# A later place for the last quarter's residual and result units of one column phase in a two-layer directional-scan kernel

## The chip, the cores and the metric

The kernel runs on one core of one Trainium2 chip. The metric is the device time of one launch in microseconds. The profile is of one execution on the chip, and all times within it are counted from the start of its span.

## What is computed

The input x has 32 images, 48 channels, 64 rows and 128 columns in float32. Two layers follow one another. Each is `x = x + conv(gn(x))`, where `gn` normalises each image over 16 groups of channels, and `conv` is four scans one behind the other. A scan goes over the rows downward, then upward, and then over the columns to the right and to the left. Each of its steps adds to the next row (or column) a 5-tap convolution of the one before it:

```python
def _conv1d(x, w, b):                      # over one row or column: 48 channels in, 48 out, 5 taps
    y = jax.lax.conv_general_dilated(x, w, window_strides=(1,), padding=[(2, 2)], ...)
    return y + b[None, :, None]
def step(w, b):
    def f(carry, inp):
        nxt = inp + _conv1d(carry, w, b)
        return (nxt, nxt)
    return f
_, d_rest = jax.lax.scan(step(down_w, down_b), d0, xs[1:])        # down the rows
_, u_rest = jax.lax.scan(step(down_w, down_b), u0, seq)           # and up
_, r_rest = jax.lax.scan(step(right_w, right_b), r0, ws[1:])      # along the columns
_, l_rest = jax.lax.scan(step(left_w, left_b), l0, R[Ww - 2::-1]) # and back
...
x = x + _L0_conv_ref(_gn(x), ...)
x = x + _L1_conv_ref(_gn(x), ...)
```

## The kernel before

**Groups and phases.** The 32 images are four groups of eight. A phase is one pair of scans: "rows" (down and up, 126 steps) for one group, or "cols" (right and left, 254 steps) for a pair of groups at a time. Twelve phases follow one another, numbered from 0:

```python
PHASES = (
    ("rows", 0, 0), ("rows", 0, 1), ("cols", 0, 0), ("rows", 0, 2),
    ("rows", 1, 0), ("rows", 0, 3), ("cols", 0, 1), ("rows", 1, 1),
    ("rows", 1, 2), ("rows", 1, 3), ("cols", 1, 0), ("cols", 1, 1),
)
```

The triple is kind, layer, and group or pair. Phase 6 is the column phase of layer 0 for the second pair (groups 2 and 3). Phase 7 is the row phase of layer 1 for group 1, and phase 8 that of layer 1 for group 2.

**A step.** `step` (L889, L898) issues nine matmuls on TensorE into three PSUM tiles, and three instructions on VectorE that add bias and input. The three tiles are the three thirds `o` of the 384 values (48 channels of eight neighbouring lines) in which a row or column is laid over the 128 partitions. A step needs the one before it. The names of the PSUM tiles tell the phase: `step_01l` is phase 6's scan to the left, `step_11d` phase 7's scan downward, `step_11u` its scan upward, `step_12d` phase 8's scan downward.

**Memory.** The tile `arena` has three slots and four staging tiles of 128 x 2048 (1 MB each). A row phase uses two slots of 32 rows. A column phase needs four quarters of 32 columns, `quarter(k, j)`, in three slots: j = 3 and j = 0 share a slot, and j = 0 goes to device memory for a while (`spill_unit`). A quarter consists of six units of 1 MB, `UNITS[i] = (o, half)`; the half is the group of the pair.

**What goes beside a column phase's end.** After the scan to the left has passed a quarter, each unit of layer 0 goes through: `load_residual` (DMAs on SP's queue, `arena<-xin`, three or four for 1 MB), `add_residual` (L824, GpSimd), `keep_result` (SP's queue, `mid<-arena`), and the statistics for the next layer's normalisation. These are `bn_stats` on VectorE (L573, eight to a unit) for half 0, and sums on ScalarE (L597, L600, L603) for half 1. The four staging tiles take the residuals in turn, so the load of unit u uses the tile of unit u - 4. When the last unit is through, `scaling` turns the statistics into scale and offset: a chain of small instructions spread over steps, with a square root on ScalarE (L469) and a reciprocal on VectorE (L479) ten steps behind it. It runs once for group 2 and, 20 steps later, once for group 3.

**What goes beside a row phase.** Rows come in four blocks of 16. `take_rows` reads them from `mid` (SP's queue, `arena<-mid`; 12, 16 and 12 DMAs for the thirds o = 0, 1, 2 of a block, 1 MB each), and `scale_rows` (L722) applies scale and offset on ScalarE, 24 activations to a block. In phase 7 block reads are due 30, 14 steps before and 2, 18 steps after its start (thirds three steps apart), and the scaling 13 steps before and 3, 19, 35 after. Rows go back to memory as `upb<-arena`. Phase 7 also loads the weights of layer 1's column scans (`more_weights`: memsets on GpSimd L323, then DMAs `taps`, `early`, `wleft`) from its 50th step on.

**Order.** All of this is put on an agenda by `at(t, fn, ...)`, where t counts steps of the whole program. Between the steps the agenda is emptied up to the current step, and `in_order` chains each instruction to the one before it on the same engine. So the agenda fixes the order on every engine and every queue; it does not fix the time, since an engine or queue goes on as soon as what it waits for is there. In `plan_cols`, `left` is the step at which the scan to the left begins and `end = left + 127` the phase's end, which is the next phase's start. The agenda of the units is made in the loop over `direct`, from the list `units` of (step, quarter, unit).

Of the kernel before, what the change touches and what calls it, by code (L numbers as in the profile page):

```python
# [119 lines left out]
def kernel(  # L120
# [631 lines left out]
    def quarter(k, j):  # L752
        return slot[slots(k)[j % 3]].rearrange("p (o s n) -> p s o n", s=2, o=NG)
# [214 lines left out]
    def at(t, fn, *args):  # L968
        agenda.append((t, len(agenda), fn, args))

    def spread(t, gen, every):


        def go(t):
            if next(gen, "end") != "end":
                at(t + every, go, t + every)
                agenda.sort(key=lambda a: a[:2])

        at(t, go, t)
# [64 lines left out]
    def follows(k):  # L1044

        _, layer, pair = PHASES[k]
        return PHASES[k - 1] == ("rows", layer, 2 * pair + 1)

    def plan_cols(k, t0, prev):
        _, layer, pair = PHASES[k]  # L1050
        n = 2 * NG
        after = prev == "cols"
        if follows(k):
            at(t0 + 1.2, hold_queue, k)
        for i in range(n):
            if follows(k) and UNITS[i][1] == 1:
                other = nc.gpsimd
                at(t0 - 31 + i, load_unit, k, 0, i, 4, NH, 0, E8, other)
                at(t0 - 13 + i, load_unit, k, 0, i, 2, 4, 0, E8, other)
                at(t0 - 6 + i / n, load_unit, k, 0, i, 1, 2, 0, E8, other)  # L1060
            else:
                early = 30 if after else 46 if k == 2 else 70
                at(t0 - early + 2 * i, load_unit, k, 0, i)
            if follows(k):
                queue = nc.sync if UNITS[i][1] else nc.scalar
                at(t0 + 1.5, load_unit, k, 1, i, 0, NH, 0, E8, queue)
            else:
                at(t0 + (3 if after else -24 + 2 * i), load_unit, k, 1, i)
            at(t0 + (38 if after else 8) + 2 * i, load_unit, k, 2, i)
            at(t0 + 33 + 2 * i, spill_unit, k, i, False)  # L1070
            at(t0 + 50 + 2 * i, load_unit, k, 3, i)
        final = k == len(PHASES) - 1
        left = t0 + W - 1
        end = left + W - 1
        for i in range(n):

            t = left + 64 + 2 * i if layer == 0 else left + 39.5 + 4.5 * i
            at(t, spill_unit, k, i, True)
        units = []
        for n_done, j in enumerate((3, 2, 1, 0)):  # L1080
            every = 4.5
            if j == 0 and PHASES[k + 1 if not final else k][0] == "rows":
                every = 7
            units += [(left + 34 + 32 * n_done + every * i, j, i) for i in range(n)]
        stats = None
        if layer == 0:
            stats = ResultStatsV(f"r{2 * pair}"), ResultStatsA(f"r{2 * pair + 1}")
        tiles = [stage[:, i] for i in range(4)]
        if layer:
            tiles += spare_tiles[0 : 2 if final else 1]  # L1090
        n = len(tiles)
        direct = [u for u in units if not (final and u[1] == 0)]

        for u, (t, j, i) in enumerate(direct):
            nat = tiles[u % n]
            o, half = UNITS[i]
            if u < n:
                at(left + 16, load_residual, k, j, i, nat)
            if layer == 0:
                if u >= n:  # L1100
                    at(direct[u - n][0] + 3, load_residual, k, j, i, nat)
                at(t, add_residual, k, j, i, nat)
                at(t + 4, keep_result, k, j, i)
                unit = quarter(k, j)[:, half, o]
                if half == 0:
                    for b in range(GB):
                        at(t + 5 + b, stats[0].take, j, o, unit, b)
                else:
                    at(t + 1, stats[1].take, j, o, unit)
            else:  # L1110

                at(t, add_residual, k, j, i, nat)
                at(t + 2.5, permute_unit, k, j, i, nat, (nc.gpsimd, nc.scalar, nc.scalar))
                if final or j not in HELD:
                    at(t + 4.5, store_result, k, j, i, nat)
                else:
                    at(t + 4.5, hold_result, j, i, nat)
                if final and j == 1:
                    at(t + 4.7, load_residual, k, 0, i, last_tiles(k)[i])

                if u >= 2 and u - 2 + n < len(direct):
                    at(t + 4.6, load_residual, k, *direct[u - 2 + n][1:], tiles[(u - 2) % n])
        if layer == 0:
            t = units[-1][0] + 14
            g = 2 * pair
            spread(t, scaling(f"r{g}", 1, g, stats[0], r_masks, 8), 1)
            spread(t + 20, scaling(f"r{g + 1}", 1, g + 1, stats[1], r_masks, 8), 1)
        if layer:

            at(left + 10, nc.scalar.copy, junk[:, BN - 1 :], quarter(k, 3)[:, 0, 0, RUN - 1 : RUN])  # L1130
        if layer and not final:
            todo = [(j, half, e) for j in HELD for half in range(2) for e in range(E8)]
            for n, what in enumerate(todo):
                at(end + 63 + 1.9 * n, let_result, *what)
        if final:
            at(end + 4, last_results, k)

    def last_tiles(k):

        s = slot[slots(k)[2]].rearrange("p (i n) -> p i n", i=2 * NG)  # L1140
        return [s[:, i] for i in range(2 * NG)]
# [13 lines left out]
    for k, (kind, layer, _) in enumerate(PHASES):  # L1155
        (plan_rows if kind == "rows" else plan_cols)(k, starts[k], PHASES[k - 1][0])
# [259 lines left out]
```

## Time and profile before

| | |
|---|---|
| runs shown | 4172.45, 4185.11, 4185.0 us; median 4185.0 us |
| profiled execution | 4178.27 us; its span 4176.5 us |
| mean granted TensorE clock | 0.989 |
| phase 6, scan to the left | first matmul 2107.8 us, last 2355.9 us |
| phase 7, scan downward | first matmul 2356.1 us, last 2496.3 us |
| phase 7, scan upward | first matmul 2496.4 us, last 2626.1 us |
| phase 8, scan downward | first matmul 2626.2 us, last 2751.6 us |
| issue to landing (median) | `arena<-xin` of 384 KB, 10.0 us; `arena<-mid` of 96 KB, 3.1 us; `mid<-arena` of 1024 KB, 10.3 us |

A view names an instruction as line, engine, operation and "tile written <- tiles read". PE is TensorE, PEld its weight loads, DVE VectorE, ACT ScalarE, POOL GpSimd, and SPq the queue of DMAs that SyncE issues. A bracket at the end of a timeline's line is the engine's idle time before it and what ended it. The view of waits gives total time, number and longest. A row of the view by stretches has, for each engine, its busy time and number of instructions, then the granted TensorE clock, the busy share of the DMA engines and their GB/s. A line of SPq in the timeline shows when a group of DMAs was issued, not when the data landed.

### The profile page before, as it was taken

Reading aid. Unit: us, or ns where it says so; the run is one execution under the profiler, and the core shown is the slowest. Engines: PE = TensorE matmul, PEld = TensorE weight load, DVE = VectorE, ACT = ScalarE, POOL = GpSimd, SP = SyncE. Lnnn points to the kernel's source line nnn. Section 1 sums busy time; section 2 is a strip of 40 time slices with the busy share of each in tenths; the row PEclk is TensorE's granted clock in tenths of the full one; section 3 lists DMA queues with packets and bytes.
Section 4 is the critical chain, followed back from the end, with each engine's and each line's share of the span. In section 5 each row is a group of like instructions: output and inputs, shape, how many; then the busy total and the mean of one; then the engine's idle time right before and its main releaser. Section 6 shows DMA issues by size and latency. Waiting matters only on the chain. (4 is left out here: it accounts for less than half of the span.)

```text
span 4176.5 us, 90284 instructions
## 1 busy us (share of the span) xinstructions
PE 4076.3 (98%) x36724; PEld 4045.9 (97%) x36724; DVE 2133.2 (51%) x6501; ACT 1287.0 (31%) x2525; POOL 787.2 (19%) x737
## 2 busy tenths in 40 slices
PE   8999999999999999999999989999999999999994
PEld 6999999999999999999999989999999999999994
DVE  5454444456654454444457654444444444444444
ACT  6844000536964543000016853413000002200122
POOL 3520010434321000010023410000000005610353
PEclk9999999999999999999999999999999999999997
DMA  9987669669979989258419968849379019999799
GB/s 294 235 178 119 111 125 213 208 161 254 217 190 163 174 157 157 37 103 201 92 45 267 188 143 139 140 74 148 57 136 212 2 51 239 287 268 155 146 236 195
DMA packets 2206496, 680.57 MB, mean 163 GB/s; under 512 B 2008464, under 2 KB 2157184, under 8 KB 2179968
## 3 DMA queue, kind: packets, MB, share of 16 engines
q1 hardware_dynamic: 2062096, 582.09, 68.0%
q10 hardware_dynamic: 141424, 87.19, 8.8%
q0 software_dynamic: 2560, 5.51, 0.5%
q8 instruction: 289, 4.73, 0.5%
q14 instruction: 127, 1.04, 0.1%
HBM read 397.77 MB, written 295.14 MB: 166 GB/s over the span
## 5 line engine op out<-in xcount | busy, mean ns | idle before, releaser
L722 ACT ACTIVATE arena<-arena,offset,scale 128x256 f32<-128x256 f32 (+2 forms) x840 | 581.3, 790 | 318.8 <-DMA arena<-mid 125.0
L824 POOL TENSOR_TENSOR arena<-arena 128x2048 f32<-128x2048 f32 x80 | 362.9, 4549 | 1447.1 <-PE step_10l L889 462.3
L659 POOL COPY arena<-arena 128x256 f32<-128x256 f32 x332 | 196.8, 659 | 455.6 <-DMA arena<-in_x 287.3
L597 ACT ACTIVATE early<-arena 128x256 f32<-128x256 f32 x192 | 129.7, 675 | 441.6 <-POOL arena L824 435.7
L889 PE MATMUL step_01r<-arena,early 128*128 128x128 f32 x2286 | 251.8, 274 | 6.8 <-DMA arena<-arena 5.5
L889 PEld LDWEIGHTS step_01r<-arena,early 128*128 128x128 f32 x2286 | 250.8, 185 | 7.7 <-issue 5.8
L889 PE MATMUL step_00r<-arena,early 128*128 128x128 f32 x2286 | 251.2, 274 | 6.9 <-DMA arena<-arena 5.4
L889 PEld LDWEIGHTS step_00r<-arena,early 128*128 128x128 f32 x2286 | 250.5, 185 | 7.6 <-issue 5.7
L889 PE MATMUL step_00l<-arena,wleft 128*128 128x128 f32 x2286 | 249.2, 272 | 0.0
L889 PE MATMUL step_11r<-arena,early 128*128 128x128 f32 x2286 | 249.2, 273 | 0.0
L889 PEld LDWEIGHTS step_11r<-arena,early 128*128 128x128 f32 x2286 | 248.7, 184 | 0.4 <-DVE arena L898 0.3
L889 PEld LDWEIGHTS step_00l<-arena,wleft 128*128 128x128 f32 x2286 | 248.7, 184 | 0.0
L889 PE MATMUL step_11l<-arena,wleft 128*128 128x128 f32 x2286 | 248.5, 272 | 0.0
L889 PE MATMUL step_10l<-arena,wleft 128*128 128x128 f32 x2286 | 248.5, 272 | 0.0
L889 PE MATMUL step_01l<-arena,wleft 128*128 128x128 f32 x2286 | 248.4, 272 | 0.0
L889 PE MATMUL step_10r<-arena,early 128*128 128x128 f32 x2286 | 248.4, 272 | 0.0
L889 PEld LDWEIGHTS step_11l<-arena,wleft 128*128 128x128 f32 x2286 | 248.4, 184 | 0.0
L889 PEld LDWEIGHTS step_10l<-arena,wleft 128*128 128x128 f32 x2286 | 248.4, 184 | 0.0
L889 PEld LDWEIGHTS step_10r<-arena,early 128*128 128x128 f32 x2286 | 248.4, 184 | 0.0
L889 PEld LDWEIGHTS step_01l<-arena,wleft 128*128 128x128 f32 x2286 | 248.4, 184 | 0.0
L282 ACT COPY early<-arena 128x1 f32<-128x1 f32 x2 | 0.4, 191 | 704.2 <-DVE arena L898 704.2
L846 ACT COPY arena<-arena 128x256 f32<-128x256 f32 x172 | 99.8, 657 | 365.5 <-POOL arena L824 249.2
(200 smaller groups left out, 7080.5 us busy)
## 6 DMA issues: line engine op xcount, KB each, us to landing
xin<-arena SPq DMA_DIRECT2D x91, 512.0 KB, 4.1
arena<-in_x SPq DMA_DIRECT2D x18, 2048.0 KB, 11.9
arena<-xin SPq DMA_DIRECT2D x96, 384.0 KB, 10.0
arena<-mid SPq DMA_DIRECT2D x384, 96.0 KB, 3.1
upb<-arena SPq DMA_DIRECT2D x192, 192.0 KB, 3.9
arena<-upb SPq DMA_DIRECT2D x96, 384.0 KB, 12.5
arena<-xin SPq DMA_DIRECT2D x180, 192.0 KB, 4.3
mid<-arena SPq DMA_DIRECT2D x32, 1024.0 KB, 10.3
```

Source lines behind the costliest of these rows:

```text
L282: fn(*args)
L597: nc.scalar.activation(junk[:, 0:n], view[:, b], AF.Identity, accum_out=self.sum[:, i, j : j + 1])
L659: copy(dst[:, r, q], src[:, r0 + r, q])
L722: nc.scalar.activation(args[0], args[0], AF.Identity, bias=args[2], scale=args[1])
L824: eng.tensor_tensor(unit, unit, nat, ALU.add)
L846: copy(by_w(perm)[:, a], src[:, a])
L889: nc.tensor.matmul(part(whole(ps[o])[0:m], -s), weights[:, i, at : at + m], part(src(i), s), start=seen[o] == 1, stop=seen[o] == left[o],)
```

## The change

Only the last quarter (j = 0) is concerned, and only where a row phase follows and `pair` is 1: phase 6. Its units' adds had been due 7 steps apart from step `left + 130`, which is 3 steps after the phase's end. Now they are due 6 steps apart from `end + 29`. What hangs on that step moves along: the keeping 4 steps later, the statistics, and the chain that makes scale and offset. A load into a staging tile was due 3 steps after the tile's previous use; now it is due no earlier than 21 steps ahead of its own add.

```diff
         units = []
         for n_done, j in enumerate((3, 2, 1, 0)):
-            every = 4.5
+            first, every = left + 34 + 32 * n_done, 4.5
             if j == 0 and PHASES[k + 1 if not final else k][0] == "rows":
-                every = 7
-            units += [(left + 34 + 32 * n_done + every * i, j, i) for i in range(n)]
+                first, every = (end + 29, 6) if pair else (first, 7)
+            units += [(first + every * i, j, i) for i in range(n)]
...
             if layer == 0:
                 if u >= n:
-                    at(direct[u - n][0] + 3, load_residual, k, j, i, nat)
+                    at(max(direct[u - n][0] + 3, t - 21), load_residual, k, j, i, nat)
                 at(t, add_residual, k, j, i, nat)
                 at(t + 4, keep_result, k, j, i)
...
         if layer == 0:
             t = units[-1][0] + 14
             g = 2 * pair
             spread(t, scaling(f"r{g}", 1, g, stats[0], r_masks, 8), 1)
             spread(t + 20, scaling(f"r{g + 1}", 1, g + 1, stats[1], r_masks, 8), 1)
```

The last piece is unchanged and shown because its step follows from `units`. In steps after phase 7's start, for the six units:

| | before | after |
|---|---|---|
| loads | -17, -12.5, -8, -3.5, +6, +13 | +8, +14, +20, +26, +32, +38 |
| adds | +3, +10, +17, +24, +31, +38 | +29, +35, +41, +47, +53, +59 |
| kept | +7, +14, ... +42 | +33, +39, ... +63 |
| scale and offset of groups 2 and 3 begin | +52, +72 | +73, +93 |

On SP's queue the order of the entries around phase 7's blocks is thereby (b3/1 is the second third of block 3):

```
before: load0 ... b2/0 load1 ... b2/1 load2 b2/2 ... load3 ... b3/0 b3/1 load4 keep0 b3/2 load5 keep1 b4/0 keep2 b4/1 b4/2 keep3 keep4 keep5 weights
after:  b2/0 ... b2/1 b2/2 ... b3/0 b3/1 load0 b3/2 load1 b4/0 load2 b4/1 b4/2 load3 load4 keep0 load5 keep1 keep2 weights keep3 weights keep4 keep5
```

The "..." in the two lines are units of the quarter before, in the same place in both.

On ScalarE the statistics of the three units of half 1 stood after block 2, after block 3 and after block 4 of the scaling, and now all stand after block 4. The square root for group 3 stood ahead of phase 8's first scaling and now stands behind its second block.

## The prediction

> **What bounds the kernel now.** I read the page first, then TensorE's waits, then the chain behind its longest wait: VectorE, ScalarE, the queue of SP.
>
> ```profile
> span 4176.5 us, 90284 instructions
> PE 4076.3 (98%) x36724; PEld 4045.9 (97%) x36724; DVE 2133.2 (51%) x6501; ACT 1287.0 (31%) x2525; POOL 787.2 (19%) x737
> ```
>
> TensorE is busy for 98%, so a gain can only come from the 100 us in which it isn't, and from time at half clock. TensorE's waits say where those are (columns: total, times, longest):
>
> ```profile
> PE step_11d L889 <- DVE arena L898: 10.9, 1, 10.9
> PE step_00d L889 <- DVE arena L898: 8.4, 4, 3.9
> PE step_01r L889 <- DMA arena<-arena: 5.5, 1, 5.5
> ```
>
> The longest single one lies in step_11d: the downward scan of phase 7, which is the phase right behind the column phase that the diff edits. VectorE's timeline there:
>
> ```profile
> 2419.26 0.35 DVE L898 SCALAR_TENSOR_TENSOR arena<-step_11d,bd,arena 128x128 f32<-128x128 f32 x1 [0.79 <-DMA arena<-mid]
> 2430.76 0.61 DVE L898 SCALAR_TENSOR_TENSOR arena<-step_11d,bd,arena 128x128 f32<-128x128 f32 x2 [11.15 <-ACT arena L722]
> ```
>
> This is row 32 (31 steps of 2.0 us after 2356.5), the first row of the third block of 16 rows. VectorE waits for ScalarE's scaling of that block. ScalarE's timeline, three groups of eight, one for each third o of the block:
>
> ```profile
> 2398.73 6.06 ACT L722 ACTIVATE arena<-arena,offset,scale 128x256 f32<-128x256 f32 x8
> 2407.90 6.07 ACT L722 ACTIVATE arena<-arena,offset,scale 128x256 f32<-128x256 f32 x8 [3.11 <-DMA arena<-mid]
> 2424.74 5.98 ACT L722 ACTIVATE arena<-arena,offset,scale 128x256 f32<-128x256 f32 x8 [10.78 <-DMA arena<-mid]
> ```
>
> So ScalarE itself waits for the row reads. SP's queue (start, time over which the group was issued) shows what those stand behind:
>
> ```profile
> 2363.22 1.78 SPq L271 DMA_DIRECT2D arena<-xin  x4
> 2365.11 11.17 SPq L271 DMA_DIRECT2D arena<-mid  x12
> 2376.32 2.03 SPq L271 DMA_DIRECT2D mid<-arena  x2
> 2378.75 4.03 SPq L271 DMA_DIRECT2D arena<-xin  x4
> 2382.82 1.02 SPq L271 DMA_DIRECT2D mid<-arena  x2
> 2383.96 22.36 SPq L271 DMA_DIRECT2D arena<-mid  x28
> 2406.41 1.32 SPq L271 DMA_DIRECT2D arena<-xin  x3
> 2407.83 0.38 SPq L271 DMA_DIRECT2D mid<-arena  x1
> 2408.32 13.39 SPq L271 DMA_DIRECT2D arena<-mid  x12
> ```
>
> The x12 at 2408.32 is the late third (o = 2, 1 MB), landed at 2424.6. One after another, without a pause, stand residual loads (xin, 1 MB a unit), kept results (mid<-arena, 1 MB) and row reads. The queue is the bound of this stage: in these stretches the DMA engines are 95% and 92% busy, and after the stall TensorE's clock has dropped as well:
>
> ```profile
> 2356.00:2418.00 62.00, 61.94 (x561) 61.60 (x561) 39.52 (x111) 50.46 (x92) 22.63 (x5) 1.00 0.95 176
> 2418.00:2436.00 18.00, 7.07 (x44) 6.90 (x43) 2.36 (x7) 11.07 (x22) 6.13 (x4) 0.63 0.92 188
> ```
>
> (PE, PEld, DVE, ACT, POOL, then clock, DMA share, GB/s.)
>
> **What the stall costs.** Step 32 is late by 10.9 us. Steps 33 and 34 then take 3.94 and 2.78 us by VectorE's timeline, not 2.0: 1.9 + 0.8 at half clock. Together 13.6 us. Cross-check: step_11d's last VectorE instruction starts 138.9 us after its first, step_12d's 124.2; of these 14.7 us, 1.3 belong to two steps that carry statistics matmuls, which stay. The Trainium skill (TensorE: Matmul & The Clock Gate, the clock-gate part) has the half-rate state end after about 3.4 us of sustained work; that would cost half of 3.4, 1.7 us, so 12.6 in all. The trace has 2.7 after the stall; I take the trace.
>
> **The change part by part.** It touches only the last quarter (j = 0) of phase 6; pair 0 keeps every 7 steps from the old start, layer 1's column phases do not meet the condition. Nothing is added or removed; six units (6 MB in, 6 MB out) move in every queue. The "+8" below are steps after phase 7's start, 2356.5.
>
> *Loads (20 DMAs on SP).* From -17, -12.5, -8, -3.5, +6, +13 to +8, +14, +20, +26, +32, +38. The max() alters no load of the other quarters: there the tile-free time is at most 20 steps ahead of the use. Ahead of the late third stood five of these loads and the first kept unit; in the new order of SP one load stands there. So 5 MB leave. Price of 1 MB of these kinds in a stretch without row reads:
>
> ```profile
> 2258.30 5.03 SPq L271 DMA_DIRECT2D arena<-xin  x3
> ...
> 2284.57 23.44 SPq L271 DMA_DIRECT2D arena<-mid  x28
> ```
>
> Between these starts three loads and three kept units went out: 26.3 us / 6 = 4.4 us per MB. The six MB of row reads at 2499.83, alone in the queue, took 49.3 us, 8.2 per MB. The Trainium skill (DMA: Bandwidth & Descriptors, Specifications) gives a ceiling of 435 GB/s, an estimated 2.4 us per MB. By the page 5 MB are 12 us: the third lands at 2412.6, is scaled by 2418.7, and is needed at 2419.6, so the stall would only just close, with 1 us to spare. By the row they are 22 us: landed 2402.6, scaled by 2408.7, 11 us to spare. I take the row, because it is this queue with these shapes; the page's figure is the low end. ScalarE is no new bound: block 2 ends at 2381.6 if not held by data (2363.5 + 24 x 0.75), block 3 needs 18 us.
>
> *Fourth block (rows 48 on).* Needed at step 48, now 2356.5 + 47 x 2.0 = 2451, where before it had the stall's 14 us of grace. Its last third landed at 2457.9. Ahead of it now stand three loads instead of six loads and three kept units: 6 MB less, 26 us, so 2432, scaled by 2438: 13 us to spare by the row; 14 us less by the page, 2443.5, scaled by 2449.6, so 1 us. This is next in line after row 32.
>
> *Adds (6 on GpSimd, 4.55 us each).* From +3..+38 to +29..+59. GpSimd has idle time of 7 to 21 us around each now. Queued behind are the two weight memsets (1.06 us each; those weights are first used three phases on) and the copy of row 63 (needed at the end of phase 7). Nothing, as long as the loads come in.
>
> *Statistics.* VectorE takes 24 bn_stats (0.62 us) at +34.., +46.., +58.., in the idle half of a 2.0 us step as before (three 0.35 us instructions there). They wait for adds, and the scan is queued behind them. Third use: step +58 is at 2472; its load now goes out behind block 4 and one more load, about 2432 + 9 + 7 to land = 2448, added by 2457 with one add ahead of it. 15 us to spare; the first two have about 20. ScalarE's three units (13.5 us each) leave the gaps between the blocks' scaling and follow block 4: 2438 + 40 = 2478; their next reader comes at +93, about 2542. Nothing.
>
> *Kept results (8 DMAs on SP).* From +7..+42 to +33..+63. One now stands behind the first set of weight DMAs (25 + 5), two units behind the second, where before all stood ahead of both. Phase 8's first read waits for the last even unit to land: bound 0 (hidden) to about 8 us (their median landing), in a queue that is then 60 us ahead of need (below). Nothing on the path.
>
> *Coefficients of rows 2 and 3.* Both chains start 21 steps later (+73, +93). The first coefficients were ready at 2534.7; minus 13.6 plus 21 steps, 2563. Phase 8's scaling began at 2572.0 before, held by the second square root, so it isn't later. The second square root now stands behind two blocks of phase 8's scaling on ScalarE (48 x 0.743 = 36 us, so until 2599), and VectorE's reciprocal that needs it moves from 2591 to 2591 - 13.6 + 42 = 2619. 20 us to spare.
>
> *Sum.* 10.9 + 2.7 = 13.6 us gained, nothing given back. The profiled execution took 4178.3 us (span 4176.5): 4164.7. The median of the three runs is 4185.0, 6.7 above it, the lowest 4172.5 below it. If the median run has the same stall, 4171.4; if its excess is a longer stall of this same queue, 4164.7. I say 4168.
>
> **The rivals.**
> *The wait moves to row 48, or only shrinks (0.14).* For it: block 4 has no grace any more, and the DMA engines stay saturated. Were the row reads slow for themselves and not by what is queued ahead, block 4 would land at 2457.9 as before, be scaled by 2464 and stop row 48 for 13 us: no change, 4178 to 4185. Half of that gives a gain of 7. Against it: reads alone run at 8.2 us per MB, 13.4 among residuals.
>
> *The square root behind the scaling (0.12), slower.* Place: VectorE's reciprocal for row 3's coefficients at step 3 of phase 8, in front of every scan step. If block 2 of phase 8 is scaled after 2619, each us later is one us of TensorE's time, plus 2.7 for the clock. It decides against the change from 2619 + 11 = 2630 on, that is, if that block lands after about 2624. For it: the kept units now stand right ahead of these reads, and other waits could add to it. Against it: those reads landed by 2550.8. A landing 25 us beyond that point: about 4178 + 25 = 4203.
>
> *No effect in a run (0.05)*, if runs outside the profile don't stall here at all: the lowest run, 4172.5, is 12.5 under the median, nearly the price of this stall. Then 4172 to 4185.
>
> **How the numbers follow.** The stall gone: 0.69, 4158 (lowest run less 13.6 = 4158.9) to 4172. Moved, shrunk or without effect: 0.19, 4172 to 4186. Slower: 0.12, 4190 to 4205. A measurement of this kernel tells about 0.3%, 12.5 us, from no change: faster is under 4172.5. The main case lies there, 0.69; the second within 0.3%, 0.19; slower 0.12. The range, 4156 to 4181, holds the main case and more than half of the second, 0.8 in all, with 2 us below the lowest sum for the spread between runs.
>
> **What would show it.** Right: TensorE's waits hold no step_11d of over 2 us; the clock in 2418 to 2436 stays at 1.00; step_11d spans about 125 us; row reads of phase 7 follow each other in SP's queue with at most one load among the third block; ScalarE scales three blocks without statistics between them. Wrong: a wait of step_11d at about 2451 (row 48), of VectorE on GpSimd's adds at about 2425, 2449 or 2472, or of step_12d within its first steps on ScalarE's square root.

## The result, and the profile after

The changed kernel takes 4165.7 us in the median (4160.2 to 4172.8, 7 runs); the kernel before, timed with it, 4185.0 us (4172.5 to 4192.4, 7 runs). The ratio is 0.9966, with a 95% interval of 0.9952 to 0.998: 14 us less, between 8 and 20. (The two medians lie 19 us apart, near the upper end of that.) Two more measurements of the same file, each beside new runs of the kernel before, gave 0.9970 (0.9959 to 0.9981) both times.

The profiled execution took 4172.8 us, 5.5 less than the profiled one of before, and not 14. The reason has to be sorted out first. TensorE's instructions of phase 7's scan downward (with the shortest, median and longest matmul in ns, and the first and last start in us):

```profile
L889 PE MATMUL step_11d<-arena,early x1134: 266/275/377, 2364.0 to 2489.4; 128*128 128x128 f32 x126, 128*96 128x120 f32 x63
```

The upward scan behind it:

```profile
L889 PE MATMUL step_11u<-arena,early x1134: 266/275/356, 2489.5 to 2620.5; 128*128 128x128 f32 x126, 128*96 128x120 f32 x63
```

The scan downward spans 125.4 us; before it was 140.2 (2356.1 to 2496.3). The upward one spans 131.0, before 129.7, since the 1.3 us of the first statistics matmuls moved into it. From phase 7's first matmul to its last it is 256.5 us against 270.0: **13.5 us gained**.

But phase 7 began 7.9 us later (2364.0, not 2356.1). The change touches nothing ahead of phase 6's last 17 steps, and in the profiles of kernels that are alike up to there this start lies anywhere from 2355.3 to 2364.0. The 7.9 us arise far ahead of the change, in two scans: from its first matmul to the next scan's, phase 2's scan to the right (`step_00r`) takes 257.5 us, before 252.5, and phase 3's scan downward (`step_02d`) 136.0, before 132.8. In the nine profiles in which both are untouched they take anything from 252.5 to 259.5 and from 127.7 to 136.0, whichever kernel it is, and every other scan ahead of phase 7 varies by less than 1 us. From phase 7's end to the end of the span the two profiles agree within 0.1 us. So the two profiled executions' times hide more than half of the gain, and the stretch that the change touches shows it.

No wait of TensorE in step_11d is left. Where its longest waits were, the list now has (total, times, longest; 7.4 us of the second line is a wait of phase 3, which was 4.1 us in the profile before):

```profile
PE step_00d L889 <- DVE arena L898: 9.7, 4, 4.0
PE step_02d L889 <- issue: 8.3, 2, 7.4
PE step_00r L889 <- DMA arena<-arena: 6.0, 3, 4.7
PE step_01r L889 <- DMA arena<-arena: 5.9, 1, 5.9
```

SP's queue in the same stage, over the times at which each group was issued:

```profile
2346.85 18.36 SPq L271 DMA_DIRECT2D arena<-mid  x28
2365.31 5.02 SPq L271 DMA_DIRECT2D mid<-arena  x4
2370.44 19.77 SPq L271 DMA_DIRECT2D arena<-mid  x28
2390.26 1.37 SPq L271 DMA_DIRECT2D arena<-xin  x3
2391.74 11.48 SPq L271 DMA_DIRECT2D arena<-mid  x12
```

The row reads of blocks 2 and 3 (x28 is two thirds, x12 the last) now have only one residual load among them. ScalarE scales block 2 and the first two thirds of block 3 in one go, and then waits for the rest:

```profile
2371.44 29.83 ACT L722 ACTIVATE arena<-arena,offset,scale 128x256 f32<-128x256 f32 x40
2405.12 6.06 ACT L722 ACTIVATE arena<-arena,offset,scale 128x256 f32<-128x256 f32 x8 [3.85 <-DMA arena<-mid]
...
2442.28 6.05 ACT L722 ACTIVATE arena<-arena,offset,scale 128x256 f32<-128x256 f32 x8 [1.75 <-DMA arena<-mid]
```

Block 3's last third is scaled from 41.1 us after phase 7's first matmul (2405.12 - 2364.0); before it was 68.6. (Six further profiles have the same order of entries around phase 7, namely those of the last two sets below; there it is scaled from 44.0 to 46.1 us on. So one profile tells this time to some us only.) Row 32 is due there after about 63.5 us, so this scaling must start by 57.5. The last line is the last third of block 4, done at 2448.3, some 11 us before row 48 needs it; in the six further profiles it is done 6 to 7 us before. The DMA engines are as busy as before, and the clock stays up:

```profile
2364.00:2426.00 62.00, 61.94 (x562) 61.60 (x561) 31.01 (x95) 49.09 (x75) 9.11 (x3) 1.00 0.96 163
2426.00:2444.00 18.00, 17.99 (x165) 17.83 (x164) 11.93 (x33) 7.78 (x11) 4.50 (x1) 1.00 0.96 142
```

These are the two stretches shown for before, moved by phase 7's later start. The second now has 18.0 us of TensorE in 18, not 7.1. The DMA engines move no more GB/s than before (163 and 142, then 176 and 188), so the wait did not go because transfers became faster; they came in another order.

### The profile page after: what moved, and what is told of

Read it like the earlier page. It is cut to its first block, busy times and chain, and to the rows that moved or that the text cites. A ratio compares the mean times of both kernels' runs of the same rounds, so it can differ in the third digit from the quotient of the medians.

```text
span 4171.0 us, 90280 instructions
## 1 busy us (share of the span) xinstructions
PE 4073.2 (98%) x36724; PEld 4042.8 (97%) x36724; DVE 2135.8 (51%) x6501; ACT 1287.2 (31%) x2525; POOL 786.9 (19%) x737
## 5 line engine op out<-in xcount | busy, mean ns | idle before, releaser
L889 PE MATMUL step_00r<-arena,early 128*128 128x128 f32 x2286 | 252.5, 274 | 9.8 <-DMA arena<-arena 6.0
L846 ACT COPY arena<-arena 128x256 f32<-128x256 f32 x172 | 99.6, 657 | 363.0 <-POOL arena L824 272.8
## 6 DMA issues: line engine op xcount, KB each, us to landing
arena<-xin SPq DMA_DIRECT2D x96, 384.0 KB, 10.2
```

The source lines that it names most:

```text
L846: copy(by_w(perm)[:, a], src[:, a])
L889: nc.tensor.matmul(part(whole(ps[o])[0:m], -s), weights[:, i, at : at + m], part(src(i), s), start=seen[o] == 1, stop=seen[o] == left[o],)
```

## The experiments

Each kernel was timed beside the kernel before on the same chip. "After phase 7's first matmul" is counted in each kernel's own profile.

**How much each MB costs, and of which kind: loads back in their old place.** From the changed kernel:

```diff
-                    at(max(direct[u - n][0] + 3, t - 21), load_residual, k, j, i, nat)
+                    at(direct[u - n][0] + 3, load_residual, k, j, i, nat)
```

> The changed kernel, but the loads of the last quarter's residuals go out where they did before (3 steps after their tile's previous use): four of them ahead of blocks 2 and 3 of phase 7's row reads. Adds, kept units and statistics stay late, so load 5 and the first kept unit (2 MB) have left the place ahead of block 3's last third, and four loads (4 MB) are back in it. Theory (each MB ahead of a row read delays it by 4.4 us, whatever it is): that third lands 8.8 us earlier than in the kernel before, the wait of step_11d for row 32 is about 2 us, not 10.9, and not 0; no wait at row 48. Rival (only loads count, or only what is issued after the phase's start counts): wait near 10.9, or none and the third landed as early as in the changed kernel. Time: between the two kernels, 8 to 13 us under the kernel before.

Measured: 4171.9 us, ratio 0.9983 (0.9973 to 0.9993). TensorE's waits in phase 7, and the scaling of block 3's last third:

```profile
PE step_11d L889 <- DMA arena<-mid: 2.2, 1, 2.2
```

```profile
2420.70 6.02 ACT L722 ACTIVATE arena<-arena,offset,scale 128x256 f32<-128x256 f32 x8 [1.47 <-DMA arena<-mid]
```

That is 59.9 us after the first matmul (2360.8), 8.7 earlier than in the kernel before, where 8.8 were expected, and the wait is 2.2 us, where 2 were. (The view of TensorE's waits names a DMA here; VectorE's timeline has 2.46 us of waiting for ScalarE's scaling at this place.) The ratio allows a gain of 3 to 11 us; 8 to 13 were expected.

**Only the kept units late.** From the kernel before:

```diff
-                at(t + 4, keep_result, k, j, i)
+                late = j == 0 and pair
+                at(end + 33 + 6 * i if late else t + 4, keep_result, k, j, i)
```

> The kernel before, in which the last quarter's six kept units of phase 6 alone are written late (33 to 63 steps into phase 7); loads, adds and statistics as before. One MB leaves the place ahead of block 3's last third, three the place ahead of block 4. Theory: the third lands 4.4 us earlier, the wait for row 32 is 6 to 7 us and still costs the clock; 4 to 5 us faster. Rival (the writes are what holds up the row reads): the wait falls to under 2 us, and the whole 13 us are gained.

Measured: 4178.2 us, ratio 0.999 (0.9981 to 1.0). TensorE waits once in phase 7:

```profile
PE step_11d L889 <- DVE arena L898: 4.6, 1, 4.6
```

```profile
2420.47 6.00 ACT L722 ACTIVATE arena<-arena,offset,scale 128x256 f32<-128x256 f32 x8 [5.43 <-DMA arena<-mid]
```

The last third is scaled from 62.3 us after the first matmul (2358.2), 6.3 earlier. So one MB brought more than the 4.4 expected, and the wait is 4.6, not 6 to 7; but the writes alone are not what held the reads up. The scan downward spans 132.9 us, 7.3 less than before; the ratio of the times allows a gain of 0 to 8 us.

**Half the delay.** From the changed kernel:

```diff
-                first, every = (end + 29, 6) if pair else (first, 7)
+                first, every = (end + 15, 6) if pair else (first, 7)
```

> The changed kernel with half the delay: adds from 15 steps into phase 7, not 29; loads then at -6, 0, +6, +12, +18, +24 steps, kept units from +19, statistics of half 1 on ScalarE at +22 and +34, ahead of block 4's scaling. Theory: three MB less ahead of block 3's last third, no wait for row 32; but only two MB less ahead of block 4, and two units of statistics (27 us of ScalarE) between block 3's and block 4's scaling: block 4 is scaled at about 2463 us (counted as in the profile before), needed at 2451: the wait moves to row 48, about 10 us plus the clock's 2.7, and 0 to 3 us are gained. Rival (any delay past the phase's start is enough): no wait, as fast as the changed kernel, 13 us under the kernel before.

Measured: 4181.5 us, ratio 0.9998 (0.9989 to 1.0008): the whole gain is gone. TensorE's waits in phase 7, and VectorE's timeline where it stands:

```profile
PE step_11d L889 <- DVE arena L898: 10.1, 1, 10.1
```

```profile
2466.90 0.61 DVE L898 SCALAR_TENSOR_TENSOR arena<-step_11d,bd,arena 128x128 f32<-128x128 f32 x2 [10.28 <-ACT arena L722]
```

This is not row 32, which no longer waits (its last third is scaled from 54.4 us on, first line below), but row 48: 105.6 us after the first matmul at 2361.3. The wait moved to the next block, at its expected size. ScalarE scaled block 4 there without a break behind two units of statistics:

```profile
2415.67 6.05 ACT L722 ACTIVATE arena<-arena,offset,scale 128x256 f32<-128x256 f32 x8 [8.86 <-DMA arena<-mid]
...
2449.02 17.85 ACT L722 ACTIVATE arena<-arena,offset,scale 128x256 f32<-128x256 f32 x24
```

So two possible causes stood in the same place, and one more kernel takes one of them away.

**Half the delay, but ScalarE's statistics behind block 4.** From the kernel just shown:

```diff
-                    at(t + 1, stats[1].take, j, o, unit)
+                    late = j == 0 and pair
+                    at(max(t + 1, end + 36) if late else t + 1, stats[1].take, j, o, unit)
```

> The kernel with half the delay (adds from 15 steps into phase 7), in which only ScalarE's statistics of the last quarter's units go behind block 4's scaling. There the wait had moved to row 48 (10.1 us), with both ScalarE's statistics and the row reads ahead of it. Theory (the queue alone decides): block 4's last third lands as late as before (about 96 us after phase 7's first step), its scaling ends 6 us later, and the wait at row 48 stays at 8 to 10 us. Rival (ScalarE's statistics between the blocks are what made it late): the wait falls under 3 us and 8 us or more are gained.

Measured: 4182.1 us, ratio 0.9995 (0.9986 to 1.0004). ScalarE is free, and the wait is the same:

```profile
2444.12 6.06 ACT L722 ACTIVATE arena<-arena,offset,scale 128x256 f32<-128x256 f32 x8 [6.14 <-DMA arena<-mid]
2457.28 5.97 ACT L722 ACTIVATE arena<-arena,offset,scale 128x256 f32<-128x256 f32 x8 [7.11 <-DMA arena<-mid]
```

```profile
PE step_11d L889 <- DVE arena L898: 10.3, 1, 10.3
```

The last third of block 4 is scaled from 99.9 us on, in the half-delayed kernel from 99.6. So the reads alone are enough for the wait, and the statistics had filled a time in which ScalarE would have waited for them. The converse, early reads with the statistics still in between, was not run: in the half-delayed kernel ScalarE was not free before 2449.0, and that alone would have ended its scaling as late.

**The loads on another queue.** From the kernel before:

```diff
-    def load_residual(k, j, i, nat):
+    def load_residual(k, j, i, nat, queue=None):
...
-                dma(nat[p0 : p0 + c1 - c0], x_by_col(t, e, j)[c0:c1])
+                dma(nat[p0 : p0 + c1 - c0], x_by_col(t, e, j)[c0:c1], queue)
...
-                    at(direct[u - n][0] + 3, load_residual, k, j, i, nat)
+                    queue = nc.gpsimd if j == 0 and pair else None
+                    at(direct[u - n][0] + 3, load_residual, k, j, i, nat, queue)
```

> The kernel before, with its steps, but the last quarter's residual loads of phase 6 go out on GpSimd's queue, not on SP's. The same MB move at about the same time over the same DMA engines, but no load stands ahead of a row read in SP's queue. Theory (the DMA engines' time is what the row reads lack): the row reads are shared out with the loads, block 3's last third lands at most some us earlier, and the wait for row 32 stays at 5 to 11 us; 0 to 5 us faster. Rival (the order in SP's queue is what holds them up): the wait goes, and 12 to 14 us are gained without any delay of the units. Loads that come late for the adds could be a cost of their own: GpSimd would then wait, and VectorE's statistics behind it.

Measured: 4182.6 us, ratio 1.0006 (0.9996 to 1.0015): no gain. But the wait is at another place than expected. The waits in phase 7, VectorE's timeline where the longest stands, and SP's queue just ahead of it:

```profile
PE step_11d L889 <- DMA mid<-arena: 14.4, 1, 14.4
```

```profile
2401.66 0.61 DVE L898 SCALAR_TENSOR_TENSOR arena<-step_11d,bd,arena 128x128 f32<-128x128 f32 x2 [14.65 <-ACT arena L722]
```

```profile
2310.57 30.34 SPq L271 DMA_DIRECT2D arena<-mid  x12
...
2343.56 27.85 SPq L271 DMA_DIRECT2D arena<-mid  x12
```

The same two groups in the kernel before:

```profile
2310.01 13.13 SPq L271 DMA_DIRECT2D arena<-mid  x12
...
2328.84 16.93 SPq L271 DMA_DIRECT2D arena<-mid  x12
```

The wait is at row 16, 14.4 us; VectorE's timeline shows that it is for ScalarE's scaling of block 2 (the first view names a DMA). GpSimd issued the loads as soon as their tiles were free (from 2308.5 on), ahead of SP's place for them, and while they ran the two groups of twelve row reads took 30.3 and 27.9 us, not 13.1 and 16.9. From 2310 to 2341 us the view of the DMA queues has (packets, MB, share of the 16 engines):

```profile
q0 software_dynamic: 544, 3.15, 51.0%
q1 hardware_dynamic: 8449, 2.89, 48.3%
```

The first line is GpSimd's queue, the second SP's, which in the kernel before had 99.8% in the same stretch and moved 7.3 MB. At row 32 only 1.4 us of waiting were left. So taking the loads out of SP's queue does not take them out of the row reads' way: both queues draw on the same DMA engines, and here each got half of them. As the view says, GpSimd's queue is of another kind than SP's; a second queue of SP's kind was not tried.

Five of the kernels in one table (time counted from phase 7's first matmul). The scaling of block 3's last third must start by about 57.5 us for row 32 not to wait:

| kernel | MB fewer ahead of that third | scaled from, us | wait at row 32, us | wait at row 48, us | step_11d, us |
|---|---|---|---|---|---|
| before | 0 | 68.6 | 10.9 | 0 | 140.2 |
| keeps late | 1 | 62.3 | 4.6 | 0 | 132.9 |
| loads early | 2 | 59.9 | 2.2 | 0 | 127.5 |
| half the delay | 3 | 54.4 | 0 | 10.1 | 138.4 |
| changed kernel | 5 | 41.1 | 0 | 0 | 125.4 |

Each wait at row 32 is the third's start less 57.5, within 0.3 us. The last column closes too: 125.4 us, the wait, what the half-rate clock costs behind it (2.7, 1.7, 0 and 2.4 us in the first four rows) and, in the first, second and in half in the fourth row, 1.3 us of statistics matmuls. A MB less is worth 4.4 to 6.3 us by these rows (4.5 to 5.5 with the further profiles of the changed order, for its five MB). The one kept unit brought 6.3 us, the three loads between the third and the last row 14 to 19; a difference between the kinds does not show beyond the spread of single profiles.

**The same idea for the first pair.** Phase 3 has a wait at row 48 of its own, 4.1 to 7.4 us in eight of the nine profiles with this phase untouched and 1.7 us in the ninth (the loads on GpSimd's queue). (The expectation below puts it at 4 to 8 us in every profile.) Its staging tiles are wanted soon by the next input, so the full delay was not tried. Two kernels made block 4 of the row reads due earlier; the first also wrote the kept units later. From the changed kernel, the second hunk only in the first of the two:

```diff
-            ahead, scaled = (-28, -12, 4, 20), (-13, 3, 19, 35)
+            fourth = 20 if PHASES[k][1] else 10
+            ahead, scaled = (-28, -12, 4, fourth), (-13, 3, 19, 35)
...
-                at(t + 4, keep_result, k, j, i)
+                late = j == 0 and not pair
+                at(end + 26 + 6 * i if late else t + 4, keep_result, k, j, i)
```

> The changed kernel, and the same idea for the first pair, whose tiles are wanted too soon for the full delay: block 4 of phase 3's row reads is due 10 steps into the phase, not 20, and phase 2's last six kept units are written 26 to 56 steps into it, not 7 to 42. So one load and two kept units (3 MB, 13 us at 4.4 us each) leave the place ahead of block 4. Phase 3's scan downward (step_02d) has a wait of 4 to 8 us at row 48 for ScalarE's scaling of that block in every profile so far, plus 2 to 4 us at half clock. Theory: the wait goes, step_02d falls from 131 to 134 us to about 126; 5 to 8 us under the changed kernel. Rival (the wait moves to the late fifth load, whose add VectorE or GpSimd then holds, or to row 32): no gain against the changed kernel.

> The changed kernel with block 4 of phase 3's row reads due at step 10, but the kept units of phase 2 where they were. One load and one kept unit (2 MB, 9 us) leave the place ahead of block 4. Theory: most or all of the wait at row 48 goes (4 to 8 us), step_02d about 126 to 128 us; 4 to 8 us under the changed kernel. Rival: the writes matter more than their MB, and more than half of the wait stays.

> The changed kernel as it is, beside the others on the same chip. Theory: 12 to 15 us under the kernel before (ratio about 0.9967), no wait of step_11d over 1 us, step_11d 125 to 126 us long; the start of phase 7 differs from profile to profile by some us, since the phases ahead of it are untouched and their waits vary.

Measured: 4168.7 us, ratio 0.9966 (0.9953 to 0.9978), and 4167.0 us, 0.9961 (0.9948 to 0.9973). The changed kernel beside them: 4170.4 us, 0.9970 (0.9959 to 0.9981). The wait at row 48 was gone in both, and step_02d, 133.3 us in the changed kernel here, spanned 127.2 and 127.8. Yet no gain can be told: the upward scan, step_02u, spanned 136.2 and 134.3 us instead of 129.6, which takes back all of it in the first kernel and most of it in the second. New waits stood there. In the second kernel:

```profile
PE ps_r L385 <- POOL dev_r L450: 2.7, 1, 2.7
```

GpSimd's timeline shows why:

```profile
1225.86 4.72 POOL L659 COPY arena<-arena 128x256 f32<-128x256 f32 x8 [14.05 <-issue]
1230.54 0.23 POOL L450 TENSOR_TENSOR dev_r<-dev_r 128x24 f32<-128x24 f32 x1
```

The short instruction of the statistics (L450) stands behind GpSimd's copies of the next input, and those are paced by that input's loads, not by steps. With the scan 6 us earlier, the statistics' matmul came too early for it. In the first kernel VectorE waited 5.1 us more, for L625 behind the next copies.

**With the chain of scale and offset 8 steps later for the first pair.** Both kernels again, with

```diff
-            t = units[-1][0] + 14
+            t = units[-1][0] + (14 if pair else 22)
```

> The kernel e5_phase3 (block 4 of phase 3 due earlier, the first pair's last kept units late), in which the first pair's chain for scale and offset begins 8 steps later (60 and 80 steps into phase 3, not 52 and 72). In e5_phase3 the wait at row 48 was gone, but step_02u had new ones (at its steps 5 and 20 to 22, 6 us in all): TensorE's and VectorE's part of that chain waited for GpSimd instructions (L450, L619 to L625) that stand behind GpSimd's copies of the next input (L659), which wait for that input's load. Theory: 8 steps, 16 us, are more than those waits, so step_02u falls to about 128 us with no step over 3.4 us, and 5 to 7 us are gained against the changed kernel (ratio to the kernel before about 0.9952). Rival (the chain's place is not what made them late): the waits return, and the time stays at the changed kernel's.

> The kernel e7_phase3_block (block 4 of phase 3 due earlier, kept units as they were) with the same 8 steps for the chain. Theory: the wait at step 5 of step_02u (4.4 us) goes, 5 to 7 us under the changed kernel, as e9_phase3_chain: the kept units' place matters little once block 4 is early. Rival: the late fifth load, now behind block 4 and the kept units, holds GpSimd and the next input's copies, and something new waits.

> The changed kernel as it is, beside the two on the same chip: 12 to 15 us under the kernel before, with the wait of 4 to 8 us at row 48 of phase 3 still there.

Measured: 4162.9 us, ratio 0.9953 (0.9939 to 0.9966), and 4162.5 us, 0.9955 (0.9941 to 0.9968). The changed kernel beside them: 4169.5 us, 0.9970 (0.9959 to 0.9981). Phase 3's downward scan in the second kernel:

```profile
L889 PE MATMUL step_02d<-arena,early x1134: 266/275/335, 1091.8 to 1216.1; 128*128 128x128 f32 x126, 128*96 128x120 f32 x63
```

It spans 124.3 us, against 135.2 in the changed kernel of the same set, and its upward scan 130.5 with no wait of TensorE, against 129.7; 1.3 us of statistics matmuls moved from the one into the other. Both kernels are about 7 us under the changed kernel, in the medians and in the ratios, though the intervals of the ratios overlap by 3 to 4 us. Whether the kept units are late as well makes no difference that shows. This is the best version found: the change, plus block 4 of phase 3 ten steps earlier, plus the first pair's chain eight steps later.

## Why the prediction was right

The forecast was 4168 us, within 4156 to 4181; 4165.7 were measured. The signs named for it came: no wait in step_11d, the clock at 1.00, 125.4 us, one load among the third block's reads, three blocks scaled without statistics between them.

- *What bounds.* Row 32's wait for the row reads, and these behind loads and kept units in a full queue: shown by the table above, in which the wait shrinks with each MB taken out, and by the half delay, where it returns one block later.
- *What the stall costs.* 13.6 us were expected between the phase's ends and 13.5 measured. 2.7 of them came from the half-rate clock, which lasted 5.3 us past TensorE's restart.
- *Loads.* 4.4 us per MB gave 22 us for five; the third came 27.5 us earlier in this profile, 5.5 per MB, and 22.5 to 24.6 earlier in the six further ones. The term was right, or a little small, on the safe side. The ceiling of 435 GB/s in the Trainium skill (DMA: Bandwidth & Descriptors, Specifications), an estimated 2.4 us per MB, is not what this queue works at: by it one MB less would have left a wait of 8.5 us, and 4.6 were measured.
- *Block 4.* 13 us to spare were expected; about 11 are there in this profile, 6 to 7 in the six further ones. Six MB less brought 19 to 24 us at this place, not 26, so this term was too large, and the margin was thinner than it looked. The rival in which the wait moves to row 48 is real: with half the delay it took the whole gain.
- *Adds and statistics.* Nothing, as measured: no wait of VectorE on an add. The fifth unit's add ended 95 us after the first matmul, expected 101.
- *Coefficients and the square root behind the scaling.* Scale and offset were there at 2570.6, 206.6 us after the first matmul, expected 206.9. ScalarE's timeline after:

```profile
2570.63 35.72 ACT L722 ACTIVATE arena<-arena,offset,scale 128x256 f32<-128x256 f32 x48 [21.62 <-POOL offset L487]
2607.44 0.22 ACT L469 ACTIVATE std_r<-var_r 128x24 f32<-128x24 f32 x1 [1.09 <-DVE var_r L467]
```

The two blocks ended at 2606.3, and the root then waited 1.1 us for its own input. So ScalarE's new order cost nothing, with VectorE's reciprocal 20 us away. The slower rival did not come near its point.

- *The sum's base.* 4164.7 from the profiled execution, 4171.4 from the median: 4165.7 lies between. That 4168 is so near is partly luck, since medians of the same file differ by some us: the two later measurements gave 4170.4 and 4169.5, against 4184.5 and 4182.4 for the kernel before. There the median less 13.6 would be 4170.9 and 4168.8, so the size of the gain does not rest on luck. The spread from profile to profile sits in `step_00r` and `step_02d`, as shown above. The first holds one wait of about 5 us in some profiles and in the others a second one of about 4 us as well, with 3.4 us or more at half clock behind it; why the second comes and goes stays open.

## What to carry to other kernels

Where a transfer queue is full, ask of each entry not whether it is early enough but what stands behind it that is due sooner; a unit whose result is not needed soon can cost the time of its transfers at another place. The loads' lead over their own adds, 20 to 28 steps before and 21 after, was not the point; the whole unit could wait. Look at the next place before choosing the length of a delay: half of this one moved the wait one block on and kept its price. And when a scan gets faster, look for work beside it that is paced by something else, such as the next input's loads, because its fixed step may now be too early. Making phase 7's row reads due earlier, as was done for phase 3, would be another way to the same order; it was not tried.

## What the runs showed of the hardware

- The price of a wait in clock depends on its length. Behind the wait of 2.2 us the granted clock stayed at 1.00. With that of 4.6 us it was at half for 3.4 us, with those of 10.1 and 10.3 us for 10.2 us, and with those of 10.9 and 14.4 us for 13.7 us. The half-rate time began 2.5 to 5.0 us after TensorE had stopped and ended 3.2 to 5.3 us after it went on; only what lies behind the restart costs time. With the kept units alone late, TensorE went on at 2427.0, and all of the half-rate time lay behind that (2427.4 to 2430.8), at a price of 1.7 us; the clock is the third number from the end:

```profile
2422.00:2427.00 5.00, 0.37 (x4) 0.21 (x3) 0.49 (x2) 5.00 (x9) 0.32 (x1) 1.00 1.01 180
2427.00:2431.00 4.00, 4.00 (x22) 4.00 (x23) 1.17 (x4) 3.84 (x12) 4.00 (x1) 0.57 1.01 149
```

- Loads issued on GpSimd's queue slowed row reads on SP's to about half their rate (30.3 us for twelve, not 13.1), although nothing more stood ahead of them in SP's own queue: GpSimd's queue had 51.0% of the DMA engines, SP's 48.3%.
